# Second message-passing pass of a GNN kernel: where the second half's norm and output stand in the instruction order

## The chip, the core and the metric

The kernel runs on one core of a Trainium2 chip. A core has five engines that each work through their own queue of instructions in order: TensorE (PE, matrix products), VectorE (DVE), ScalarE (ACT), GpSimd (POOL) and SyncE (SP), which here issues DMAs. [...] The metric is the device time of one launch in microseconds. The kernel before takes 2396.82 us, the median of three runs from 2393.73 to 2397.0.

## The reference, cut to what matters

Sixteen graphs of 1024 nodes with 128 features each go through a gated layer (four rounds of a GRU), a row norm, then a pruning of the adjacency (`_dilate`), three SAGE layers with a batch norm behind each, a linear head and a last row norm. The change lies in the second of the three SAGE layers:

```python
def _sage(x, adj, Wr, Wx, b, mf):
    deg = jnp.clip(jnp.sum(adj, axis=-1, keepdims=True), 1.0, None)
    agg = jnp.einsum('bij,bjd->bid', adj, x) / deg
    out = agg @ Wr + x @ Wx + b
    nrm = jnp.maximum(jnp.linalg.norm(out, axis=-1, keepdims=True), NORM_EPS)
    return out / nrm * mf[..., None]
def _bn(x, g, b):
    m = jnp.mean(x, axis=(0, 1))
    v = jnp.var(x, axis=(0, 1))
    return (x - m) * jax.lax.rsqrt(v + BN_EPS) * g + b
...
h1 = _bn(jax.nn.relu(_sage(x, adj_d, Wr1, Wx1, b1, mf)), g1, be1)
h2 = _bn(jax.nn.relu(_sage(h1, adj_d, Wr2, Wx2, b2, mf)), g2, be2)
h3 = _bn(jax.nn.relu(_sage(h2, adj_d, Wr3, Wx3, b3, mf)), g3, be3)
```

In the text, r is `relu(out / nrm * mf)` of one layer, before its batch norm. The batch norm runs over all graphs, so a pass must have finished r of every graph before the next layer's weights exist.

## The kernel before

The kernel has stages one after the other: the gated layer beside the pruning, then the three SAGE passes `first`, `second`, `third`, and the head. The order of the instructions on all five engines is the order in which the Python code issues them (a manual schedule); what a line issues first runs first on its engine.

`second` walks over the graphs b = 0 to 16 in turns of eight slots, t = 0 to 7, and calls `slot_second(b, t)` (line 1775) for each. A graph's 1024 rows are treated as two halves f = 0 and 1 of 512 rows. In turn b two graphs are in work. For graph b, the output of the second SAGE layer is made; for graph b - 1 (named `p` in the code), the aggregation that the third layer needs is made from r. The pieces:

- `out_next` (1752), t = 0 and 3: TensorE's products for half f into the PSUM tiles `q_oa` (lines 1758) and `q_ob` (1761, 1764).
- `chain` (1767), t = 0 and 3: VectorE scales the rows and adds (1381, 1382), giving `s_o`; ScalarE squares the rows with a running sum and takes the root (1389, 1390), giving `s_ss`. Line 1811 adds to the accumulator of the head.
- `rows` (1393): four VectorE instructions, the maximum with 1e-12 (1395), the reciprocal (1396), the mask (1397), and `relu(o) * s` (1400), giving r in the tile `s_r`. For half 0 it is at t = 2 of the graph's own turn, for half 1 at t = 0 of the next turn.
- `split` (1403): r is split for the products into a rounded part `q_rh` (ScalarE, 1405) and its rest `q_rl` (GpSimd, 1406). Half 0 at t = 3 of the own turn, half 1 at t = 0 of the next.
- `turn_r` (1592): TensorE transposes r (1411, PSUM tile `s_tr`), ScalarE copies it out (1597, `s_rt`), VectorE takes the statistics for the batch norm (1598). Half 0 at t = 4 of the own turn, half 1 at t = 1 of the next; a DMA then stores `s_rt`.
- The aggregation of graph b - 1 (line 1800, PSUM tiles `q_ag0` and `q_ag1`): for f = 0 eight products with `q_rh` at t = 1 and eight with `q_rl` at t = 2, for f = 1 at t = 4 and 5. At t = 3 and 6 ScalarE copies it out (`evict`, 1567, tile `s_ag`) and a DMA stores it.
- `unpack` (1740): the adjacency comes as bytes (`q_b`) and is unpacked to float32 in eight slices of 128 x 1024, the tiles `q_at0` and `q_at1` (one buffer each). Slices are issued at the end of t = 3, 4, 5, 6, 7 of the own turn and t = 0, 1, 2 of the next, by GpSimd, ScalarE, GpSimd, VectorE, and the same again for the second tile.

What stands behind the moved lines in their queues: on VectorE the statistics of half 0 and the slice of t = 6; on ScalarE the eviction of t = 6; on GpSimd the slice of t = 7. On SP, the loads for the next graph but one stand behind the store of that eviction. The tiles `s_r`, `s_o`, `q_rh`, `q_rl` and `s_rt` have two buffers, `s_tr` and `q_oa` one.

Of the kernel before, what the change touches and what calls it, by code (L numbers as in the profile page):

```python
# [22 lines left out]
B = 16  # L23
# [1173 lines left out]
class Sage:  # L1197
# [577 lines left out]
    def slot_second(self, b, t):  # L1775
        nc, g, p = self.nc, self.g.get(b), self.g.get(b - 1)
        acc = lambda b, f: self.acc[:, b, 4 * f:4 * f + 4, :]
        if b < B:
            if t == 1:
                self.load_second(b + 1)  # L1780
                self.load_bytes(b + 1, 0)
            if t == 3:
                self.load_bytes(b, 1)
            if t in (0, 3):
                self.out_next(b, t // 3, self.ps1)
        if p is not None:
            if t == 0:
                p["r", 1] = self.rows(b - 1, 1, p.pop(("o", 1)), p.pop(("ss", 1)))
                self.split(1, p["r", 1], p["rh"], p["rl"])
            if t == 1:  # L1790
                self.turn_r(1, b - 1, 1, self.ps1)
                if b < B:
                    nc.sync.dma_start(self.rt[b - 1, 1], p["rt", 1])
            if t in (1, 2, 4, 5):
                f = t // 4
                if t in (1, 4):
                    p["pa", f] = self.ps1.tile([C, HF], F32, name=f"q_ag{f}")
                part = p["rh"] if t in (1, 4) else p["rl"]
                for j in range(NB):
                    nc.tensor.matmul(p["pa", f], part[:, j, :], p["at", f][:, j, :],  # L1800
                                     start=(t in (1, 4) and j == 0), stop=(t in (2, 5) and j == NB - 1))
            if t in (3, 6):
                f = t // 6
                p["ag", f] = self.evict(p["pa", f], b - 1, f)
                if b < B:
                    nc.sync.dma_start(self.ag[b - 1, f], p["ag", f])
        if b < B:
            if t in (0, 3):
                f = t // 3
                pp = self.chain(b, f)  # L1810
                nc.vector.tensor_add(acc(b, f), pp, g["x"][:, 4 * f:4 * f + 4, :])
            if t == 2:
                g["r", 0] = self.rows(b, 0, g.pop(("o", 0)), g.pop(("ss", 0)))
            if t == 3:
                g["rh"] = self.wk.tile([P, NB, C], FR, name="q_rh")
                g["rl"] = self.wk.tile([P, NB, C], FR, name="q_rl")
                self.split(0, g["r", 0], g["rh"], g["rl"])
            if t == 4:
                self.turn_r(1, b, 0, self.ps1)
                nc.sync.dma_start(self.rt[b, 0], g["rt", 0])  # L1820
        if t >= 3:
            if b < B:
                self.unpack(b, t - 3)
        elif p is not None:
            self.unpack(b - 1, t + 5)
        if t == 7 and b < B:
            self.g.pop(b - 1, None)

# [211 lines left out]
```

## Time and profile before

| what | value |
|---|---|
| three runs | 2396.82, 2393.73, 2397.0 us |
| profiled execution, span | 2393.6 us |
| TensorE busy in the span | 2269.3 us (95%) |
| VectorE busy | 1924.3 us (80%) |
| ScalarE busy | 1373.5 us (57%) |
| GpSimd busy | 1014.7 us (42%) |
| second pass, first product to last `q_ag` | 1907.4 to 2177.3 us |
| period of one graph in it | 15.92 us |

The profile is one execution, and its times count from the start of it. Shares of busy time are averages over stages with different limits; what a wait is worth has to be read in the stage where it stands. Of a wait the profile tells who waited, in which line, and whose instruction ended it. Matmuls are pipelined, so that the busy time of TensorE overstates its work: the distance from the start of one group of matmuls to the start of the next is the safer measure.

### The profile page before, as it was taken

What the parts mean: (1) busy time and instruction counts of PE and PEld (TensorE: products, weight loads), DVE (VectorE), ACT (ScalarE), POOL (GpSimd) and SP (SyncE); (2) the same over time, 40 slices, a digit from 0 to 9 for tenths busy, and PEclk for the clock granted to TensorE, in tenths of its full rate; (3) what the DMA queues carried; (4) which work ended last, traced back from release to release, by engine and by line L of the source; (5) the groups of instructions that cost most, each with busy time, mean ns of one, the idle gap of its engine ahead of it and who ended that gap; (6) DMA issues with size and microseconds to landing.
All of it is one profiled execution on the core that took longest, in us unless ns stands there. A gap on an engine that the chain in (4) does not pass through costs nothing.

```text
span 2393.6 us, 35727 instructions
## 1 busy us (share of the span) xinstructions
PE 2269.3 (95%) x11945; PEld 1561.1 (65%) x11945; DVE 1924.3 (80%) x4130; ACT 1373.5 (57%) x3209; POOL 1014.7 (42%) x963
## 2 busy tenths in 40 slices
PE   6999999999999999999999599999999889998987
PEld 4666555656556656656666377777777777776865
DVE  4998998989989989989899777877777466665876
ACT  3556565665565656565746466566666444545756
POOL 3235253353362543533622356666666344441001
PEclk9999999999999999999999799999999999999999
DMA  7337254364271553533630868777877366664414
GB/s 260 111 98 262 69 191 146 115 230 132 95 246 60 176 185 119 186 132 119 231 101 31 315 237 295 280 258 282 300 277 269 116 215 232 242 207 147 143 45 134
DMA packets 214394, 436.18 MB, mean 182 GB/s; under 512 B 59574, under 2 KB 80728, under 8 KB 214200
## 3 DMA queue, kind: packets, MB, share of 16 engines
q1 hardware_dynamic: 186756, 345.96, 41.9%
q0 software_dynamic: 23040, 83.90, 10.2%
q10 hardware_dynamic: 4400, 3.95, 0.5%
q8 instruction: 96, 1.57, 0.3%
q14 instruction: 102, 0.80, 0.1%
HBM read 324.49 MB, written 109.25 MB: 181 GB/s over the span
## 4 chain that ended last, share of the span: by engine, by line
PE 58%; DVE 16%; ACT 10%; DMA 9%; issue 4%; POOL 3%; SPq 0%; DVEq 0%; ACTq 0%; POOLq 0%
PE h_g L1092 15%; PE h_g L1080 12%; PE p_ag L1561 9%; DMA e_sum<-h_x 3%; DVE f_rank L735 3%; ACT s_junk L1389 3%; PE q_ag L1800 3%; PE p_u L1482 2%; PE p_u L1489 2%; PE p_u L1488 2%; DMA h_a<-in_adj_dram 2%; PE q_ob L1764 2%; PE s_tr L1411 1%; DVE s_o L1382 1%; PE u_p L1890 1%
## 5 line engine op out<-in xcount | busy, mean ns | idle before, releaser
L1092 PE MATMUL h_g<-h_h,h_wh 128*128 128x512 f32 x768 | 397.7, 599 | 3.4 <-DVE h_r L1105 3.3
L1092 PE MATMUL h_g<-h_ms,h_wi 128*128 128x512 f32 x768 | 392.2, 592 | 0.0
L1497 POOL CAST p_b<-p_at 128x512 uint8<-128x512 f32 x256 | 251.7, 1003 | 139.8 <-ACT p_at L1490 131.3
L735 DVE TENSOR_TENSOR_SCAN f_rank<-f_a,f_first,f_pd 128x1024 f16<-128x1024 f32 x128 | 299.1, 2342 | 3.3
L1080 PE MATMUL h_g<-h_a,h_hi 128*128 128x512 f32 x1024 | 284.8, 418 | 6.4 <-DMA h_a<-in_adj_dram 6.3
L1490 ACT ACTIVATE p_at<-p_u,s_less 128x512 fp32r<-128x512 f32 x256 | 175.7, 687 | 160.0 <-PE p_u L1489 155.1
L1092 PEld LDWEIGHTS h_g<-h_ms,h_wi 128*128 128x128 f32 x768 | 145.6, 190 | 183.9 <-issue 161.6
L1121 POOL TENSOR_TENSOR h_h<-h_zh,h_r 128x512 f32<-128x512 f32 x126 | 182.0, 1444 | 194.9 <-DVE h_r L1120 172.8
L1080 PE MATMUL h_g<-h_a,h_lo 128*128 128x512 f32 x1024 | 264.2, 395 | 0.0
L1080 PEld LDWEIGHTS h_g<-h_a,h_hi 128*128 128x128 f32 x1024 | 188.4, 188 | 71.0 <-issue 20.1
L863 DVE SCALAR_TENSOR_TENSOR f_nr<-f_u,f_q,f_a 128x1024 bf16<-128x1024 f16 x128 | 183.7, 1451 | 57.2 <-ACT f_u L912 50.6
L1115 POOL TENSOR_TENSOR h_zh<-h_z,h_h 128x512 f32<-128x512 f32 x63 | 80.4, 1276 | 323.8 <-ACT h_z L1111 323.8
L1080 PEld LDWEIGHTS h_g<-h_a,h_lo 128*128 128x128 f32 x1024 | 190.0, 188 | 39.3
L1506 DVE SCALAR_TENSOR_TENSOR p_a<-p_a 128x1024 bf16<-128x1024 f32 x128 | 209.4, 1674 | 3.1 <-DMA p_a<-in_adj_dram 3.1
L1092 PEld LDWEIGHTS h_g<-h_h,h_wh 128*128 128x128 f32 x768 | 129.1, 190 | 86.6 <-issue 67.3
L1389 ACT ACTIVATE s_junk<-s_o 128x128 bf16<-128x128 f32 x384 | 113.7, 298 | 109.3 <-DVE s_o L1382 109.3
L1083 ACT COPY h_ms<-h_g 128x512 f32<-128x512 f32 x128 | 73.7, 576 | 175.2 <-PE h_g L1080 131.2
L1108 ACT ACTIVATE h_r<-h_r,h_bi 128x512 f32<-128x512 f32 x128 | 92.3, 721 | 138.7 <-DVE h_r L1107 138.7
L1488 PE MATMUL p_u<-ident_b,p_a 128*128 128x128 bf16 x1024 | 144.7, 221 | 13.8 <-DMA p_a<-in_adj_dram 13.8
L909 ACT ACTIVATE f_u<-f_rank,f_q 128x128 f16<-128x128 f16 (+7 forms) x128 | 110.6, 867 | 75.2 <-DVE f_rank L849 75.2
L1489 PE MATMUL p_u<-ident_b,p_nr 128*128 128x128 bf16 x1024 | 144.7, 221 | 0.0
L1764 PE MATMUL q_ob<-s_wxp,q_xt 128*128 128x256 f32 x512 | 130.8, 399 | 0.0
(258 smaller groups left out, 4956.8 us busy)
## 6 DMA issues: line engine op xcount, KB each, us to landing
h_a<-in_adj_dram POOLq DMA_DIRECT2D x128, 512.0 KB, 7.4
p_a<-in_adj_dram SPq DMA_DIRECT2D x128, 512.0 KB
f_a<-in_adj_dram SPq DMA_DIRECT2D x124, 512.0 KB
e_nr<-f_nr SPq DMA_DIRECT2D x128, 256.0 KB
p_nr<-e_nr SPq DMA_DIRECT2D x32, 1024.0 KB
s_at<-p_b SPq DMA_DIRECT2D x32, 512.0 KB
s_ag<-s_ag SPq DMA_DIRECT2D x64, 256.0 KB
q_agi<-s_ag SPq DMA_DIRECT2D x32, 512.0 KB
```

The costliest lines, as they stand in the source:

```text
L735: nc.vector.tensor_tensor_scan(out, a, other[:, 0, 0:1].to_broadcast([P, N]), start, op0=ALU.add, op1=ALU.bypass)
L863: nc.vector.scalar_tensor_tensor(nr, self.us[g], self.q[:, 2, g:g + 1], self.a[g], op0=ALU.not_equal, op1=ALU.is_ge)
L1080: nc.tensor.matmul(pm[f], part[:, j, :], st.adj[j][:, half[f]], start=(j == 0 and n == 0), stop=(j == NB - 1 and n == 1))
L1092: nc.tensor.matmul(pg, lhs, rhs, start=(i == 0), stop=(i == len(mm) - 1))
L1121: aid.tensor_tensor(h, zh, r, ALU.subtract)
L1389: self.nc.scalar.activation(junk, o[:, i, :], AF.Square, accum_out=ss[:, i:i + 1])
L1488: nc.tensor.matmul(pu[:, i * P:(i + 1) * P], a[:, blk, 1], ib, start=False, stop=False)
L1489: nc.tensor.matmul(pu[:, i * P:(i + 1) * P], nr[:, k, blk], ib, start=False, stop=(i == 3))
L1497: self.nc.gpsimd.tensor_copy(g["b", f][:, j, :], g["at"][:, j, f * HF:(f + 1) * HF].bitcast(F32))
L1506: self.nc.vector.scalar_tensor_tensor(low, a, 0.0, a, op0=ALU.is_gt, op1=ALU.not_equal, accum_out=self.bad[:, c:c + 1])
L1561: self.nc.tensor.matmul(pa, hi[:, j, :], at[:, j, f * HF:(f + 1) * HF], start=(start and n == 0), stop=(stop and n == len(js) - 1))
L1764: nc.tensor.matmul(pb[:, i], g["xt"][:, f, blk], self.wxp, start=False, stop=(i % 2 == 1))
```

## The change

Two calls for half 1 move from the next graph's turn into the graph's own turn. `rows` for half 1 is now issued at t = 4, in front of `turn_r` of half 0 (so in front of that half's statistics on VectorE). `split` for half 1 is now issued at t = 5, behind the slice that is unpacked there. Both calls at t = 0 of the next turn go. The transposes of half 1 stay at t = 1 of the next turn, so TensorE's queue has the same order as before, and so has SP's.

```diff
         if p is not None:
-            if t == 0:
-                p["r", 1] = self.rows(b - 1, 1, p.pop(("o", 1)), p.pop(("ss", 1)))
-                self.split(1, p["r", 1], p["rh"], p["rl"])
             if t == 1:
                 self.turn_r(1, b - 1, 1, self.ps1)
...
             if t == 4:
+                g["r", 1] = self.rows(b, 1, g.pop(("o", 1)), g.pop(("ss", 1)))
                 self.turn_r(1, b, 0, self.ps1)
                 nc.sync.dma_start(self.rt[b, 0], g["rt", 0])
         if t >= 3:
...
         elif p is not None:
             self.unpack(b - 1, t + 5)
+        if t == 5 and b < B:
+            self.split(1, g["r", 1], g["rh"], g["rl"])
```

## The prediction

> **What bounds the kernel now.** I read the views in this order: the page's chain of waits (which engine carries the end), the list of waits inside the stage that the change touches (1944 to 2160 us, fourteen graphs in step), the same chain in order of time, and the timeline of one graph. All times are microseconds from the start of the profiled execution.
>
> The page gives TensorE (PE) the largest share of the chain:
>
> ```profile
> PE 58%; DVE 16%; ACT 10%; DMA 9%; issue 4%; POOL 3%; SPq 0%; DVEq 0%; ACTq 0%; POOLq 0%
> ```
>
> In the second pass the only steady wait of TensorE is this one, fourteen times in fourteen graphs; the other is its mirror on ScalarE:
>
> ```profile
> ACT q_rh L1405 <- DVE s_r L1400: 47.4, 14, 3.4
> PE s_tr L1411 <- DVE s_r L1400: 10.8, 14, 0.8
> ```
>
> (Columns: waited in total, times, longest.) The transposes of r's second half (`s_tr`, line 1411) wait for `rows` (line 1400). The chain in time shows why r is late; columns are start, length, what:
>
> ```profile
> 2032.35 0.70 DVE s_o L1382
> 2033.07 1.29 ACT s_junk L1389 x8
> ...
> 2035.01 0.59 ACT s_rt L1597
> ...
> 2036.23 0.79 DVE q_at L1750
> 2037.02 0.93 DVE s_ss L1395
> 2037.98 0.19 DVE s_ss L1396
> 2038.19 0.74 DVE s_ss L1397
> 2039.02 1.42 DVE s_r L1400
> 2040.43 0.14 issue
> 2040.57 0.63 PE s_tr L1411 x4
> ```
>
> The sums of squares end near 2034.6, but VectorE (DVE) first waits for the copy `s_rt`, does its statistics, unpacks a slice of `q_at`, and only then comes to the four instructions of `rows`, which take 0.93 + 0.19 + 0.74 + 1.42. The timeline says what they collide with:
>
> ```profile
> 2034.38 0.21 ACT L1390 ACTIVATE s_ss<-s_ss 128x4 f32<-128x4 f32 x1
> 2035.18 1.30 POOL L1406 TENSOR_TENSOR q_rl<-s_r,q_rh 128x512 fp32r<-128x512 f32 x1 [7.65 <-ACT q_rh L1405]
> 2036.42 3.46 POOL L1750 CAST q_at<-q_b 128x1024 fp32r<-128x1024 uint8 x3
> 2037.81 1.99 PE L1764 MATMUL q_ob<-s_wxp,q_xt 128*128 128x256 f32 x8
> 2039.02 1.41 DVE L1400 SCALAR_TENSOR_TENSOR s_r<-s_o,s_ss 128x512 f32<-128x512 f32 x1
> 2040.57 0.63 PE L1411 MATMUL s_tr<-ident,s_r 128*128 128x128 f32 x4 [0.76 <-DVE s_r L1400]
> ```
>
> GpSimd (POOL) runs three unpacking casts from 2036.42 to 2039.88, exactly while `rows` runs. For the first half's r, with GpSimd idle, the same four take 0.15, 0.18, 0.16 and 0.69 (from 2029.52).
>
> **What the skill says.** "SBUF — State Buffer", section "Who interferes with whom": a VectorE instruction with two SBUF inputs, or in a two-port mode, and a GpSimd instruction that reads SBUF exclude each other for a whole instruction, and whoever starts first wins. The trace agrees: line 1400 takes 1.41 against 0.69, 1397 0.72 against 0.16, 1395 1.00 against 0.15, while 1396, with one input, keeps 0.18. "TensorE: Matmul & The Clock Gate", section "What's actually happening": TensorE's clock halves after an idle window of about 3.4 us and returns after as long a busy one. The trace agrees: the granted clock is 0.51 from 1926 to 1932, after a wait of 4.67, and 0.64 from 2168 to 2172, after one of 4.13. "Perfetto Trace Analysis", its introduction: busy time of pipelined matmuls misleads. So I count from start to start, below.
>
> **The change part by part.** Nothing is added or removed: four VectorE, one ScalarE, one GpSimd instruction per graph move. The queues of TensorE and SyncE keep their order, so no DMA is passed in its own queue.
>
> 1. *`rows` of half 1, from the next turn to t = 4, ahead of the statistics.* It now waits for the sqrt (end 2034.59) and starts at 2034.62, GpSimd being idle until 2035.18. 1395 to 1397 take 0.62 with their gaps, so 1400 comes at 2035.24, just behind `q_rl`, which reads SBUF. Lower bound: it slips in first, 0.69. Upper: it waits until `q_rl` ends at 2036.48 and then takes 0.69. I take the upper: r is ready at 2037.2 instead of 2040.43. TensorE asks for it near 2039.6, so even the bad case has 2.4 to spare.
> What then is the wait worth? Unblocked, eight `q_ob` matmuls started at 2030.32 let the next group start at 2031.96, 1.64 later; blocked, the transposes start 2.76 after `q_ob` (2037.81 to 2040.57). Transposes behind another group start about 0.2 later than a plain matmul (the 2034.00 ones come 2.04 after eight matmuls that otherwise take 1.83). So 2.76 - 1.84 = 0.92 a graph; bounds 0.76 (the idle that the timeline shows) and 1.12. Fourteen graphs: **12.9** (10.6 to 15.7).
> 2. *The statistics, the slice of q_at at t = 6, and L1381/L1382 of the next graph now queue behind `rows`.* Statistics 2037.1 to 2037.8 (before 2035.62); the slice, possibly held by one cast, ends near 2038.9. TensorE needs that slice for its seventh `q_ag` matmul, near 2041.3: 2.4 to spare. L1381 ends near 2039.5, and L1382 must wait for `q_ob` anyway. Cost nothing, hidden by TensorE's 3.0 of `q_oa` and `q_ob`.
> 3. *`split` on ScalarE moves ahead of the eviction `s_ag` of half 1.* It cannot start before 2037.2, so `s_ag` (before 2036.49) starts near 2037.9. Behind it wait, on SP, the store of `s_ag` and the loads of a later graph, issued from 2037.5 on and now about 1.4 later; they are used a turn (some 15) later. The PSUM bank is asked for again some 10 later. Nothing.
> 4. *`q_rl` of half 1 on GpSimd moves ahead of the unpacking at t = 7.* GpSimd: `q_rl` 0 to 2036.5, VectorE's 0.69 and the slice in between, first two casts to about 2040.0, `q_rl` 1 to 2041.3. TensorE needs the second cast (its fifth matmul) near 2040.85: 0.85 to spare, the tightest place. The part in `q_rl` is asked for only near 2042.7. Nothing.
> 5. *Start of the pass.* Before, TensorE stood still 4.67 for graph 0's half 1 and then ran at half clock: its first eight `q_ag` took 3.56 start to start (against 1.94), the next 2.25. Now r is ready by 1923.4, and the cast of the first slice, behind `q_rl` and 1400, by about 1924.6, which is where `q_ag` starts instead of 1927.52: 2.9. The idle being shorter than 3.4, the clock may stay up, which is worth another 2.0 to 2.4. Between 2.5 and 5.5, I take **4.5**.
> 6. *End of the pass.* Before, 4.13 of idle and half clock. Now r of graph 15 is ready near 2164.5 and the transposes start then instead of at 2167.92, but the casts (serial on GpSimd, about 1.15 each, with two `q_rl` of 1.3) feed the last four groups: `q_ag` starts near 2165.6, waits 0.9 for the second cast, and ends near 2173.8 instead of 2177.26. I take **3.5** (3.0 to 4.5). The third pass starts from `q_ag`'s end (its loads are released by it), so this carries through.
>
> Sum: 12.9 + 4.5 + 3.5 = 20.9. Against the profiled span of 2393.6 that is 2372.7; against the median of the three times, 2396.82, it is **2375.9**. The span lies 0.1 under the lowest of the three times, so I use the median for the forecast.
>
> **Rivals.**
> - *The lock moves the wait rather than ending it* (part 4). For: 0.85 is less than one cast of 1.15, and 1400 meets `q_rl`. Against: I already put both holds in. One more cast's hold leaves about 0.5 for fifteen graphs, 7.5: 2383.4.
> - *A loop through VectorE and ScalarE takes over at the old period.* For: they carry a quarter of the chain. Against: after the move, r half 1 is ready 2.4 before it is needed and half 0 about 2. Then only the two ends gain, 8: 2388.8.
> - *Slower: the slice at t = 6 comes too late* because `rows` in front of it is held by cast after cast, so that `q_ag`'s seventh matmul waits in every graph. Place: VectorE's queue at 2035 to 2041. Before, the four lost 0.85 + 0.56 + 0.72 = 2.1 to holds. It starts to cost beyond 2.4 of further delay and eats the whole gain beyond 2.4 + 21/16 = 3.7, three more casts. With four more, 4.6, each graph loses 0.9 net, 14 over sixteen: about 2411. Against: GpSimd has only `q_rl` to run when `rows` now starts.
> - *The move does nothing*: something else holds r, and the time stays at 2396.8. Against: r's four instructions wait for nothing but the sqrt, 2.4 before they start now.
>
> **How the numbers follow.** Forecast 0.73; moved wait 0.12; VectorE loop 0.06; no change 0.03; slower 0.06. The forecast's own ends are 16.1 and 25.7 of gain: 2380.7 and 2371.1; the first rival stretches the range to 2384. About 0.2%, 4.8, is what a measurement here can tell from no change. The first two cases and most of the third are faster by more: 0.90; same 0.04; slower 0.06.
>
> **What would show it.** Right: the wait of `s_tr` on 1400 gone from the list, the period of a graph 15.0 instead of 15.92, no 4-us wait at either end, 1400 of half 1 near 1.9 with `q_rl` as the holder. Wrong: a new TensorE wait on `q_at` or `q_rl`, above all on a GpSimd cast before the fifth `q_ag` matmul, or the clock still at a half near 1926 to 1932.

## The result

The changed kernel takes 2373.69 us, the median of four runs from 2370.43 to 2378.28, against 2396.6 us for the kernel before (also four runs). The ratio is 0.9908, with a 95% interval from 0.9890 to 0.9927: 22.9 us or 0.92% faster. The forecast was 2375.9, with a range from 2371.1 to 2384.

### The profile after

The profiled span falls from 2393.6 to 2371.7 us, and TensorE's share of the chain of waits on the page grows from 58% to 63% at the cost of VectorE, ScalarE and DMA:

```profile
PE 63%; DVE 14%; DMA 8%; ACT 8%; issue 3%; POOL 3%; SPq 0%; DVEq 0%; ACTq 0%; POOLq 0%
```

The list of waits inside the second pass (1940 to 2150 us; waited in total, times, longest) shows the fourteen waits of the transposes gone. The one that is left belongs to graph 15. What VectorE waits for instead is the root, at the place where `rows` now stands:

```profile
DVE s_ss L1395 <- ACT s_ss L1390: 13.8, 14, 1.0
ACT q_rh L1405 <- DVE s_r L1400: 7.3, 14, 0.5
...
PE s_tr L1411 <- DVE s_r L1400: 0.7, 1, 0.7
```

The chain in order of time (start, length, what) over one graph holds TensorE and nothing else, where the kernel before had half of it on VectorE and ScalarE. From one set of transposes of half 1 (2029.09) to the next (2044.06) it is 14.97:

```profile
2029.09 0.44 PE s_tr L1411 x4
2029.53 3.69 PE q_ag L1797 x16
2033.21 0.89 PE q_oa L1758 x8
2034.11 0.54 PE q_ob L1761 x4
2034.64 1.92 PE q_ob L1764 x8
2036.57 1.85 PE q_ag L1797 x8
2038.42 0.44 PE s_tr L1411 x4
2038.86 1.85 PE q_ag L1797 x8
2040.71 0.89 PE q_oa L1758 x8
2041.60 0.54 PE q_ob L1761 x4
2042.14 1.92 PE q_ob L1764 x8
2044.06 0.44 PE s_tr L1411 x4
```

The timeline of a graph shows `rows` of half 1 in its new place:

```profile
2023.91 0.17 DVE L1395 TENSOR_SCALAR s_ss<-s_ss 128x4 f32<-128x4 f32 x1 [0.99 <-ACT s_ss L1390]
...
2024.47 1.30 POOL L1406 TENSOR_TENSOR q_rl<-s_r,q_rh 128x512 fp32r<-128x512 f32 x1 [7.59 <-ACT q_rh L1405]
2024.60 1.72 DVE L1400 SCALAR_TENSOR_TENSOR s_r<-s_o,s_ss 128x512 f32<-128x512 f32 x1
...
2025.71 2.94 POOL L1750 CAST q_at<-q_b 128x1024 fp32r<-128x1024 uint8 x2
...
2028.93 0.60 PE L1411 MATMUL s_tr<-ident,s_r 128*128 128x128 f32 x4
```

Line 1400 starts 0.13 us behind `q_rl` and ends 0.55 us behind its end, hence 1.72 instead of 0.69: it is held while `q_rl` runs. It is done at 2026.32, 2.6 us before the transposes. They no longer carry a wait.

At the two ends of the pass the waits are shorter, not gone. These are the transposes of half 1 of graphs 0 and 15 before,

```profile
1926.78 1.09 PE L1411 MATMUL s_tr<-ident,s_r 128*128 128x128 f32 x4 [4.67 <-DVE s_r L1400]
...
2167.92 1.09 PE L1411 MATMUL s_tr<-ident,s_r 128*128 128x128 f32 x4 [4.13 <-DVE s_r L1400]
```

and in the changed kernel:

```profile
1923.13 0.63 PE L1411 MATMUL s_tr<-ident,s_r 128*128 128x128 f32 x4 [1.27 <-DVE s_r L1400]
...
2146.25 0.63 PE L1411 MATMUL s_tr<-ident,s_r 128*128 128x128 f32 x4 [0.72 <-DVE s_r L1400]
```

Behind each of these two, `q_ag` waits twice for a cast of GpSimd, 0.9 us in all four. These waits on casts are new.

Three distances in the trace split the pass. All are between starts of groups on TensorE, but for the last end: from the first `q_oa` of the pass to the `q_oa` of graph 1's half 1 (the start), from there to the `q_oa` of graph 15's half 1 (fourteen graphs), and on to the end of the last `q_ag`.

| kernel | start | one graph | end | pass |
|---|---|---|---|---|
| before | 25.94 | 15.915 | 21.09 | 269.85 |
| changed | 20.71 | 14.973 | 17.35 | 247.69 |
| gain | 5.23 | 0.942 (13.18 in 14) | 3.74 | 22.16 |

Outside the pass the two profiles agree: it begins at 1907.4 and 1907.5, and 216.4 and 216.5 us follow it. So the difference of the spans, 21.9, comes from within it.

The start also shows a change of clock. The table by stretch (bounds, length, busy time of the engines with instructions, then granted clock, DMA share and GB/s) has this line for the kernel before,

```profile
1926.00:1932.00 6.00, 5.22 (x15) 4.30 (x16) 3.46 (x7) 3.52 (x12) 2.35 (x3) 0.51 0.71 283
```

and this one for the changed kernel:

```profile
1926.00:1932.00 6.00, 6.00 (x33) 4.97 (x32) 3.42 (x8) 3.25 (x12) 2.56 (x3) 1.00 0.73 293
```

In the same 6 us TensorE runs 33 matmuls instead of 15. The granted clock (third figure from the end) is 1.00 instead of 0.51, and the kernel before was still waiting for the first 0.8 us.

### The profile page after: what moved, and what is told of

It is laid out like the page before. It is cut to its first block, busy times and chain, and to the rows that moved or that the text cites. A ratio compares the mean times of both kernels' runs of the same rounds, so it can differ in the third digit from the quotient of the medians.

```text
span 2371.7 us, 35696 instructions
## 1 busy us (share of the span) xinstructions
PE 2262.0 (95%) x11929; PEld 1558.3 (66%) x11945; DVE 1908.9 (80%) x4130; ACT 1373.6 (58%) x3209; POOL 1022.1 (43%) x963
## 4 chain that ended last, share of the span: by engine, by line
PE 63%; DVE 14%; DMA 8%; ACT 8%; issue 3%; POOL 3%; SPq 0%; DVEq 0%; ACTq 0%; POOLq 0%
PE h_g L1092 15%; PE h_g L1080 12%; PE p_ag L1561 9%; PE q_ag L1797 5%; PE q_ob L1764 3%; DVE f_rank L735 3%; DMA e_sum<-h_x 3%; PE p_u L1488 2%; PE p_u L1489 2%; DMA h_a<-in_adj_dram 2%; PE p_u L1482 2%; PE s_tr L1411 2%; ACT s_junk L1389 2%; PE q_oa L1758 2%; PE u_p L1890 1%
## 5 line engine op out<-in xcount | busy, mean ns | idle before, releaser
L1488 PE MATMUL p_u<-ident_b,p_a 128*128 128x128 bf16 x1024 | 144.4, 221 | 13.8 <-DMA p_a<-in_adj_dram 12.8
```

The lines of the kernel that those rows point to most:

```text
L1488: nc.tensor.matmul(pu[:, i * P:(i + 1) * P], a[:, blk, 1], ib, start=False, stop=False)
```

## The experiments

The theory: before, TensorE waited for r of half 1; r was late because `rows` stood behind other work on VectorE and then met GpSimd's casts. There are six rivals: the gain comes from the ends or from the steady part alone; the parts `q_rh` and `q_rl`, not r itself, were awaited; standing in front of the statistics is what counts; the place in the queue alone counts, and not the casts; VectorE's load is what counts. In the tables below "pass" and its parts are those of the profiled execution, cut as above. They resolve more than the times, since the profiled pass starts anywhere from 1905.7 to 1909.9 us in these runs.

### Ends alone and middle alone

Only graphs 0 and 15, or only graphs 1 to 14, get the new order. The edit is shown against the changed kernel, with S written for that set:

```diff
+            if t == 0 and not (b - 1 in S):
+                p["r", 1] = self.rows(b - 1, 1, p.pop(("o", 1)), p.pop(("ss", 1)))
+                self.split(1, p["r", 1], p["rh"], p["rl"])
...
+                if b in S:
+                    g["r", 1] = self.rows(b, 1, g.pop(("o", 1)), g.pop(("ss", 1)))
...
-        if t == 5 and b < B:
+        if t == 5 and b < B and b in S:
```

> Only graphs 0 and 15 are changed, graphs 1 to 14 keep rows and split of half 1 in the next graph's turn. Theory (TensorE waits for r of half 1; the two ends lose their 4-us waits and the half clock behind them): the gain is 4.9 at the start and 3.5 to 4 at the end, about 8.6 us under the kernel before (near 2388), and the period of the graphs in between stays 15.92. Rival (the gain is the steady period alone, and the ends are swallowed by the casts of GpSimd): 0 to 2 us under before.

> Only graphs 1 to 14 are changed, graphs 0 and 15 keep the old place. Theory: 14 x 0.93 = 13 us under before (near 2383.6), the period falls to 14.97, and the waits of 4.7 and 4.1 us at the two ends stay. With the ends-only kernel the gains should add up to the whole change (about 22). Rival (the period only falls because the start leaves the pipeline in another phase): the period stays near 15.9 and the gain near 0.

| kernel | time, us | ratio to before (95%) | start | one graph | end |
|---|---|---|---|---|---|
| ends alone | 2391.05 | 0.9973 (0.9962 to 0.9984) | 21.11 | 15.939 | 17.33 |
| middle alone | 2383.67 | 0.9943 (0.9929 to 0.9956) | 25.95 | 14.973 | 22.50 |

The kernel before, run beside them, takes 2397.9. The gains, 6.9 and 14.2 us, add up to 21.1, close to the 22.9 of the whole. Both rivals fall: neither part has all of it. In the profiled passes the gains are 8.27 and 11.77, 20.0 of 22.2. Of the rest, 1.4 lies at the end of the middle alone: 22.50 against 21.09 before, with the same wait of 4.13, but with two stretches of 3.4 us at half clock behind it instead of one (0.50 from 2155.68 to 2162.51; before, from 2167.44 to 2170.85). So the gain at an end depends by about that much on how long the half clock lasts in the run that is compared. The waits on r confirm the split. With the ends alone, sixteen short ones are listed:

```profile
PE s_tr L1411 <- DVE s_r L1400: 13.1, 16, 1.3
```

With the middle alone, only the two long ones:

```profile
PE s_tr L1411 <- DVE s_r L1400: 8.8, 2, 4.7
```

### Only `rows` moves

Against the changed kernel, `split` goes back to its old place:

```diff
+            if t == 0:
+                self.split(1, p["r", 1], p["rh"], p["rl"])
             if t == 1:
                 self.turn_r(1, b - 1, 1, self.ps1)
...
-        if t == 5 and b < B:
-            self.split(1, g["r", 1], g["rh"], g["rl"])
```

> rows of half 1 is moved, split of half 1 stays in the next turn (behind the eviction on ScalarE and behind the fourth cast on GpSimd). Theory: what TensorE waited for was r for the transposes, not its parts; q_rl is then ready about 1.1 us before TensorE's fifth product with it, so the steady gain stays whole: 2372 to 2376, period 15.0, perhaps 1 to 2 us lost at the ends. Rival (the parts must move too): a wait of q_ag on q_rl of 0.5 to 1 us per graph, 2382 to 2390.

It takes 2375.77 us, 0.9914 of before (0.9899 to 0.9929). The period is 14.973, exactly that of the whole change; start and end are 21.53 and 18.13, together 1.6 longer. In the timeline of a graph `q_rl` of half 1 now comes behind three casts:

```profile
2026.73 3.93 POOL L1750 CAST q_at<-q_b 128x1024 fp32r<-128x1024 uint8 x3
...
2029.95 0.60 PE L1411 MATMUL s_tr<-ident,s_r 128*128 128x128 f32 x4
...
2030.63 1.29 POOL L1406 TENSOR_TENSOR q_rl<-s_r,q_rh 128x512 fp32r<-128x512 f32 x1
...
2032.25 1.08 PE L1799 MATMUL q_ag<-q_at,q_rl 128*128 128x512 f32 x4
```

It ends at 2031.92, before TensorE even begins with the products of `q_rl`. So r for the transposes was awaited, not its parts. The second half of the change is worth nothing in the steady part and 1.6 us of the pass at its ends, less than the times can separate (2375.77 against 2373.69).

### `rows` behind the statistics

The changed kernel with two lines exchanged:

```diff
-                g["r", 1] = self.rows(b, 1, g.pop(("o", 1)), g.pop(("ss", 1)))
                 self.turn_r(1, b, 0, self.ps1)
+                g["r", 1] = self.rows(b, 1, g.pop(("o", 1)), g.pop(("ss", 1)))
```

> As the changed kernel, but rows of half 1 stands behind the statistics of half 0 instead of in front of them. Theory: it then starts 1.6 us later, runs into q_rl and two casts of GpSimd (holds of about 0.3, 0.6 and 0.7 us), and r comes near the moment TensorE wants it: at most 0.3 us of wait per graph, 2374 to 2380. Rival (standing in front of the statistics is what brings the gain): most of the steady gain is lost, 2384 to 2390.

It takes 2378.24 us, 0.9926 (0.9911 to 0.9941), and again the period is 14.973. All that is lost lies at the ends: 23.66 at the start and 19.65 at the end, 5.3 us together. In the timeline `rows` begins 0.26 us before `q_rl` ends (at 2026.89) and then meets the casts:

```profile
2026.63 0.28 DVE L1395 TENSOR_SCALAR s_ss<-s_ss 128x4 f32<-128x4 f32 x1
...
2026.84 2.02 POOL L1750 CAST q_at<-q_b 128x1024 fp32r<-128x1024 uint8 x2
2026.95 0.18 DVE L1396 RECIPROCAL s_ss<-s_ss 128x4 f32<-128x4 f32 x1
2027.16 0.73 DVE L1397 TENSOR_TENSOR s_ss<-s_ss,mask 128x4 f32<-128x4 f32 x1
...
2028.35 1.05 DVE L1400 SCALAR_TENSOR_TENSOR s_r<-s_o,s_ss 128x512 f32<-128x512 f32 x1 [0.46 <-DVE s_ss L1397]
```

The holds are 0.13, 0.56 and 0.36 us over the free durations (0.3, 0.6 and 0.7 were expected), and r, done at 2029.40, is still 0.6 us ahead of the transposes (2030.02). To be in front of the statistics is not what brings the steady gain. The move across the end of the turn is enough for it. The place in front serves graphs 0 and 15: they have the only two waits on r that are left in this kernel, 3.2 and 2.7 us.

### How much r may be late

Between lines 1397 and 1400 stand n statistics instructions for half 1 whose results nobody uses (`extra` is n there, and 0 for half 0); the rest is the changed kernel:

```diff
+        for i in range(extra):
+            spare = self.small.tile([P, 6], F32, name="s_spare")
+            nc.vector.bn_stats(spare, o.rearrange("p a b -> p (a b)"))
         sc = ss.rearrange("p (k o) -> p k o", o=1).to_broadcast([P, 4, C])
```

> The changed kernel with three extra statistics instructions (results unused) between lines 1397 and 1400 for half 1, about 1.85 us of VectorE in every graph. Theory (r has 2.4 us to spare, of which this takes about 1.4, since the first 1.1 us would have been spent waiting for GpSimd anyway): no wait of TensorE, period 15.0, within 3 us of the changed kernel (2371 to 2377). Rival (VectorE itself now limits the pass): 1.85 us more per graph, about 2403.

> The same with nine extra instructions, about 5.5 us per graph. Theory: r comes 1.5 to 2.3 us too late, TensorE's wait on line 1400 is back with that length, 25 to 37 us over the changed kernel (2398 to 2411). Rival (VectorE limits): 5.5 us per graph, about 2460. Rival (r is not what TensorE waited for): no more than 5 us over the changed kernel.

| kernel | time, us | ratio to before (95%) | start | one graph | end |
|---|---|---|---|---|---|
| n = 3 | 2376.46 | 0.9915 (0.9899 to 0.9932) | 21.11 | 14.947 | 17.30 |
| n = 9 | 2427.03 | 1.0127 (1.0110 to 1.0144) | 27.03 | 17.768 | 22.84 |

The kernel before, run beside them, takes 2395.98. Three cost nothing: the pass is 247.66 us, that of the changed kernel 247.69. Nine cost 51 us of pass (298.63 less 247.69), 39.1 in the fourteen graphs and 11.8 at the two ends. The wait is back, twelve times between 1944 and 2150 us:

```profile
PE s_tr L1414 <- DVE s_r L1403: 25.1, 12, 2.5
```

(The edit moves 1400 to 1403 and 1411 to 1414.) This is a threshold and not a slope. By the rival that VectorE's load counts, three extra instructions would cost a third of nine, and nine about 5.5 us a graph; measured are 2.8, and VectorE is busy for 13.8 us of a graph's 17.8.

The cost is larger than expected, 51 against 25 to 37. In eight of the fourteen graphs the wait is 2.5 us, where 1.5 to 2.3 were worked out, and in six it is 1.5. A graph with the longer wait and full clock takes 17.66 us from `q_oa` to `q_oa`, 2.69 over the changed kernel; fourteen of these would be 37.7. What lies beyond is for the most part the two ends, where TensorE waits 5.2 and 5.9 us (1.3 and 0.7 in the changed kernel) and runs at half clock behind that: they lose 6.3 and 5.5 us.

In some graphs the transposes themselves become slow:

```profile
2037.91 0.67 DVE L1403 SCALAR_TENSOR_TENSOR s_r<-s_o,s_ss 128x512 f32<-128x512 f32 x1
...
2038.73 1.09 PE L1414 MATMUL s_tr<-ident,s_r 128*128 128x128 f32 x4 [2.52 <-DVE s_r L1403]
```

and the table by stretch gives the granted clock (third figure from the end) around them:

```profile
2034.00:2037.50 3.50, 2.22 (x11) 1.45 (x9) 3.50 (x7) 0.00 (x0) 1.86 (x2) 1.00 0.16 62
2037.50:2041.00 3.50, 2.27 (x8) 2.01 (x9) 3.40 (x6) 1.11 (x2) 1.68 (x2) 0.63 0.12 46
```

The clock record of this trace has five stretches of 3.4 us at half clock within the fourteen graphs and none in the changed kernel's. A graph that meets one takes 19.1 to 19.3 us, but the next one only 16.6, since its wait is the short one. In the sum over fourteen graphs the half clock costs little, 39.1 less 37.7.

### The old place without the casts

The kernel before, with GpSimd's slices given to ScalarE:

```diff
-        e = "gpsimd scalar gpsimd vector".split()[t % 4]
+        e = "scalar scalar scalar vector".split()[t % 4]
```

> The kernel before, with rows and split of half 1 at their old place, but with the slices that GpSimd unpacked given to ScalarE, so that GpSimd runs no cast beside rows. It tells how much of the old wait came from the holds and how much from the place in the queue. If the holds (2.1 us in the four instructions) made r late: the four take 0.15, 0.18, 0.16 and 0.69 us, but the copy that the statistics wait for comes about 1 us later behind ScalarE's extra slices, r comes about 1 us earlier in sum, and the wait of TensorE shrinks to 0 to 0.3 us: 2378 to 2386. If the place alone matters: the wait stays near 0.8 us per graph and the time near 2396.

It takes 2382.17 us, 0.9942 of before (0.9926 to 0.9959). The period is 14.973 here too, with `rows` where it always stood. In the timeline its four instructions run at their free durations:

```profile
2028.54 0.16 DVE L1395 TENSOR_SCALAR s_ss<-s_ss 128x4 f32<-128x4 f32 x1
...
2028.74 0.18 DVE L1396 RECIPROCAL s_ss<-s_ss 128x4 f32<-128x4 f32 x1
2028.95 0.17 DVE L1397 TENSOR_TENSOR s_ss<-s_ss,mask 128x4 f32<-128x4 f32 x1
...
2029.22 0.69 DVE L1400 SCALAR_TENSOR_TENSOR s_r<-s_o,s_ss 128x512 f32<-128x512 f32 x1
```

r is done at 2029.91, 0.5 us before the transposes (2030.42). So in the steady part r came too late in the kernel before because of the old place and the 2.1 us of holds together: without the holds the old place does. The rival that the place alone matters falls. The edit is not a pure removal of the holds, since ScalarE is now busy for 11.6 us of a graph instead of 8.1; but no steady wait of TensorE is left that this could have caused. At the ends the place matters even so, 23.74 and 19.93 us, nearly as with `rows` behind the statistics.

### Casts earlier still

The changed kernel with GpSimd's slices of the first tile in front of `q_rl` of half 0:

```diff
+                self.unpack(b, 0)
+                self.unpack(b, 2)
                 self.split(0, g["r", 0], g["rh"], g["rl"])
...
-            if b < B:
+            if b < B and t not in (3, 5):
                 self.unpack(b, t - 3)
```

> The changed kernel with GpSimd's two slices of the first tile (t = 3 and 5) issued in front of q_rl of half 0. Theory: TensorE already sets the period in the middle (14.97), so nothing is gained there; at the start and the end the first products no longer wait for the casts (0.17 and 0.26 us seen at each) and line 1400 of graphs 0 and 15 is not held by q_rl for less time, so 0.5 to 2.5 us under the changed kernel. Against it: the two casts now meet rows of half 0 and hold it by up to 2 us, which has about 2 us to spare; if that is not enough, 0.3 us per graph are lost, 5 us over the changed kernel.

It takes 2374.38 us, 0.9909 (0.9893 to 0.9926), not to be told from the changed kernel. The pass is 0.72 us shorter, all of it at the ends (20.18 and 17.17; 0.5 to 2.5 was expected), and the period stays 14.973. Together with the chain above, which holds TensorE alone, this says that TensorE's own work sets the steady part now.

## Why the prediction was right

Time and sign came out as forecast, and so did the terms of the sum: 13.2 in the middle against 12.9, 5.2 at the start against 4.5, 3.7 at the end against 3.5. The middle is right by its mechanism. The two ends are right in kind, and in part by luck in size.

- **The wait and its worth.** Right. The 0.92 a graph from start to start became 0.942, where the wait listed by the profile (0.76) would have given 10.6 instead of 13.2.
- **Step 1.** The upper bound was the one to take: 1400 is held by `q_rl` (1.72; I had 1.93), and r has 2.6 us to spare against the 2.4 predicted. Three extra instructions fit into the spare time and cost nothing; nine do not, and the wait is back.
- **Step 2, nothing for the work behind `rows`.** Right: no wait of TensorE on the slice of t = 6 is in the list.
- **Step 3.** The eviction moved later as predicted: measured back from the transposes of half 1 it starts 2.1 us ahead of them, where the kernel before, with its 0.94 of extra wait taken off, has 3.1. The loads behind it follow, and nothing waits for them.
- **Step 4, the tightest place.** Too dark: the first two casts end at 2028.65, before the transposes, not 0.4 behind them. They and the holds between them take 2.94 from the end of `q_rl`, where I had 3.5. Half of the excess is the 1.15 for a cast, a third of the 3.46 for three casts in the kernel before, of which some was held already: two free casts take 2.02. TensorE's fifth `q_ag` matmul comes at 2030.30, so the second cast has 1.6 to spare and not 0.85, which left the first rival less room than I gave it.
- **Steps 5 and 6.** The mechanism is shown by the kernel with the ends alone, and the clock stayed at 1.00 from 1926 to 1932. Two errors of size cancel at the start. Counted from the start of the pass, the first `q_ag` comes 3.7 earlier (16.40 instead of 20.13), where I had 2.9; behind it 1.5 are gained, where I had 2.0 to 2.4 for the clock and nothing for the second cast, which now costs a wait of 0.26. And 0.4 of the 3.7 is there before the transposes of graph 0's half 0, where nothing was changed: the two runs differ in how long the half clock lasts with which the pass begins (to 1914.9 and 1913.4). At the end, too, the gain depends on the half clock of the run before, as the middle alone showed.
- **The 3.4 of step 5.** I counted on the clock because the idle would be shorter than 3.4. The changed kernel waits 1.27 there and keeps its clock, but the rule as I used it does not hold here: with `rows` behind the statistics, waits of 3.2 and 2.7 are each followed by 3.4 us at half clock, and with nine extra instructions waits of 2.5 were, in five cases of eight. The measurement decides.
- **The rivals.** The VectorE loop falls with the three extra instructions, and the late slice with the absence of its wait. The sign of being wrong, a new wait of TensorE on a cast, is seen at the two ends alone, 0.9 in all; in the steady part there is none.

What the prediction did not say is that two different cures would have done in the steady part. It treated the queue and the holds as one cause. The runs show that in the middle either is enough, no holds in the old place or the new place with its holds, while at the two ends the place in front of the statistics gives more than the absence of holds.

## What to carry to other kernels

When a small chain on VectorE is late, look at what runs on GpSimd in the same microseconds: two instructions on 128 x 4 elements took 1.7 us here beside casts, and 0.3 once the casts had gone from GpSimd. No semaphore stands between them and the casts, so the list of waits does not name this; only the durations show it. Work out the margin at the consumer, from start to start on the engine that waits. Once it was positive, moving the producer further up bought nothing in the steady part, only at the ends of the loop, where nothing else bridges the time.

## What was not expected

With nine extra instructions, five of the eight waits of 2.5 us were followed by half clock and three were not; none of the waits of 1.5 was, and none of those of 0.76 in the kernel before. The trace lets one see why. In the pass its clock changes only at times that lie multiples of 3.41 us apart. In the five cases TensorE is busy for only 0.88 to 1.41 us of the 3.41 before the half clock begins. In the other three more of the wait lies across a boundary between two such stretches, and none of these has less than 1.48. These are the two stretches on either side of the line, the first followed by half clock, the second not (length, then TensorE's busy time):

```profile
2000.84:2004.25 3.41, 1.41 (x9) 1.26 (x10) 3.41 (x7) 1.11 (x2) 0.82 (x1) 1.00 0.00 0
2072.52:2075.93 3.41, 1.48 (x9) 1.34 (x10) 3.41 (x7) 1.11 (x2) 0.89 (x1) 1.00 0.00 0
```

This is read from one trace, and no run tested it by moving a wait against the stretches. Nor is busy time the whole measure: in the kernel with the ends alone, where the pass ends, a stretch with 1.70 (2168.33 to 2171.74) is followed by half clock too.

GpSimd pays too for holds: two casts take 2.94 us in the changed kernel, with line 1400 and a slice of VectorE beside them, and 2.01 in the kernel with nine extra instructions, where only statistics run beside them. The statistics instruction was never held there: the 130 records of the extra ones from 1943 us on take 0.67 to 0.69 us each, beside `q_rl` and the casts or not.
